# Moving the products behind two attention loops into the loops, pair by pair, and halving the unread products

## The chip, the cores and the metric

The kernel runs on one core of a Trainium2 chip. The metric is the device time of one execution in microseconds (us). The core's engines work beside one another and wait on semaphores: TensorE (PE: matrix products and transposes, with its weight loads, PEld), VectorE (DVE), ScalarE (ACT), GpSimd (POOL) and SyncE (SP, here only the issuer of DMAs). In the profile one float32 product appears as two records on PE; a transpose as one.

## The reference

Four decoder layers over x (16 batches of 112 tokens of 256 elements; 1792 tokens in all) with a context of 375 tokens for each batch:

```python
for l in range(4):
    x = x + tanh(g_xattn[l]) * xattn_l(layernorm(x), ctx, ...)
    x = x + tanh(g_ffn[l]) * ffn_l(layernorm(x), ...)
```

Layers 2 and 3 have attention with 16 heads of 16 elements (layer 2 with rotary positions, layer 3 with a mask) and then a mixture of experts:

```python
# layer 2: attn @ Wo.T + bo; then, with xn = rms_norm(layernorm(x)) * ln_w
logits = xn @ Wg + bg                      # 8 experts, the best 2, softmax over them
y = silu(xn @ W1a_e + b1a_e) * (xn @ W1b_e + b1b_e) @ W2_e + b2_e
# layer 3: attn @ Wo.T + bo; then, with xn = layernorm(x)
scores = sigmoid(xn @ gate.T + bias)       # 9 experts, the best 2, scaled to sum 1
y = silu(xn @ w1_e.T) * (xn @ w3_e.T) @ w2_e.T
```

## The kernel before

All x stays in SBUF as 14 tiles of 128 tokens (`x`, 128 partitions by 14 by 256). `hT` holds 256 by 1792 values with the features on the partitions: normed rows before an attention, and the attention's outcome after it, in the same place. The framework schedules instructions of an engine out of program order where dependencies allow, except those that are pinned (`pinned`, `tc.keep_in_program_order`), which keep their order. Each engine then runs its queue in order.

**The loop `attention16` (L726)** serves layers 2 (tag a2) and 3 (a3). It has 64 units, four heads each of one batch, and 70 steps: step s makes the score products of unit s (`scores`, into one PSUM tile `sS` of four banks with a single buffer) and DVE takes their maxima (layer 2: one reduce; layer 3: four operations that add the mask, L770). A step later the maxima are transposed and subtracted from the queries (`maxima`, qa). `by_keys` makes the scores again, transposed, in rounds of three heads, into the PSUM tag `sT` (three banks, one buffer), and ACT takes their exponentials (L797). Four rounds fall on every three steps: where s % 3 is 1 there are two rounds, one ahead of `values` and one behind it; in other steps one, behind it. `values` works on unit s - 4, then come `by_queries`, `normalise` (sums and o on DVE) and, in even steps, `by_rows`, whose ACT copy (L830) puts 128 rows of 112 tokens into `hT`. Batch b is complete in step 4b + 8. PE's work, and the reduces on DVE, are pinned. The order of a step is written out by hand:

```python
scores(s); tasks of between[s]; by_keys(slot 0); values(s - 4); by_keys(slot 1)
by_queries(s - 4); maxima(s - 1); by_rows; normalise(s - 4); tasks of behind[s]
```

`between` and `behind` are lists of tasks by step. Before the change they hold, for steps 0 to 12 alone, what is left of the norm of the attention's own input: `moments_at` (mean and variance of tiles), `roots_at` (`inv_sqrt`, L187: 12 small DVE operations for 1/sqrt), `scaled_at` (rows minus mean, times root), `rows_at` (PE transposes of a pair of tiles, ACT copies to `hT`) and `group2`/`group3` (queries of four batches). A task of `between` takes its PSUM bank from `sT`.

**Unread products** (`spin`, L256) are products that nothing reads. They stand in six steps at the start of the loop (`spins`), in every step from 64 on (L862: six each), ahead of layer 1's experts (`spin1`), of layer 3's attention (`spin3`, `a3spin`), and in layer 3's routing (`spin4`, and L968 in `dispatch`).

**Behind the loop** `outcome` (L891) goes over groups of four tiles: outcome products with wo (`a2ops`, `a3ops`), DVE's gated add to x (L900), and `norm2` or `norm3` (statistics, root by ACT's square root and DVE's reciprocal, rows kept in `hx`, transposes and copies to `hT`). After all 14 tiles rows (and in layer 3 x) are stored to DRAM for the experts' gather, `route` (L335) makes the router's products for all tiles in one bank, and `chosen`, `softmax_of` and `dispatch` sort tokens into blocks of 256. The expert blocks follow. In layer 2 this stretch also holds 40 fillers (`fill`): keys and values of ten batches for layer 3, each with its loads and stores.

Of the kernel before, what the change touches and what calls it, by code (L numbers as in the profile page):

```python
# [21 lines left out]
P = 128  # L22
# [64 lines left out]
def flamingo_kernel(ctx, tc, a, out):  # L87
# [118 lines left out]
    def roots(n0, m, pin=free):  # L206
        inv_sqrt(rss[:, n0:n0 + m], mvs[:, n0:n0 + m, 1], LN_EPS, pin=pin)

    def norm_stats(n0, m, by_act=False, rms=False):


        moments(n0, m)
        rs, var = rss[:, n0:n0 + m], mvs[:, n0:n0 + m, 1]
        if by_act:
            up, eps = (1.0 + FEPS, FEPS * LN_EPS) if rms else (1.0, LN_EPS)
            nc.vector.tensor_scalar(rs, var, up, eps, ALU.mult, ALU.add)
            nc.scalar.activation(rs, rs, AF.Sqrt)
            nc.vector.reciprocal(rs, rs)
        else:
            roots(n0, m)  # L220
# [113 lines left out]

    def route(name, w, E):  # L335

        ps = ps_o(name)
        for n in range(NT):
            mm2(ps[:, n * E:(n + 1) * E], lambda k: hT[:, k, n * P:(n + 1) * P], w)
        return ps[:, :NT * E]  # L340
# [378 lines left out]
    def rows_at(n):  # L719
        def task(three, mm, tr):  # L720
            ps = three()
            for i in range(2):
                norm_rows(n + i, lambda _: ps[:, i, :], tr, h=hs.pop(n + i))
        return task

    def attention16(pool, pp, tag, qT, kTs, vs_, store, nm=None, maskT=None, beside=(), between=None, behind=None, spins=(0, 0)):  # L726
# [4 lines left out]
        units = 4 * NB  # L731
        oT = hT
# [108 lines left out]
        for s in range(units + 6):  # L841
# [3 lines left out]
            for i, t in enumerate((between or {}).get(s, ())):  # L845
# [15 lines left out]
            if s >= units:  # L861
                spin(mi[:, M_END:], 6, None, mm)  # L862
            for t in (behind or {}).get(s, ()):
                t()
# [25 lines left out]

    def outcome(tag, wo, g, norm):  # L891

        for n0 in range(0, NT, 4):
            m = min(4, NT - n0)
            ps = ps_pair(f"{tag}ops{n0}").rearrange("p i (j d) -> p (i j) d", j=2)[:, :m, :]
            for i in range(m):
                mm2(ps[:, i, :], lambda k: hT[:, k, (n0 + i) * P:(n0 + i + 1) * P],
                    lambda k: wo[:, k, :])
            xs = x[:, n0:n0 + m, :]
            nc.vector.scalar_tensor_tensor(xs, ps, g, xs, ALU.mult, ALU.add)  # L900
            norm(n0, m)
            fill()
# [38 lines left out]
    def dispatch(pool, keep, tag, one, two, gates, n_e):  # L941
# [25 lines left out]
        if not filler:  # L967
            spin(ps_o(f"{tag}spin")[:, :w], 40, tot.rearrange("p e n -> p (e n)"))  # L968
# [460 lines left out]
    both = const.tile([P, NT, 16], F32, name="both")  # L1429
# [124 lines left out]
    spin(ps_pair("spin1")[:, 0, :], 16)  # L1554
    for n in added:
        normed(n, 1, ps_pt)
    for n in turned + added:
        route1(n, ps_o)
# [79 lines left out]
    wo = w3(w_l2o, 0, D)  # L1638
    with tc.tile_pool(name="l2x", bufs=2) as pool:
# [4 lines left out]
        with tc.tile_pool(name="a2ps", bufs=1, space=PSUM) as pp:  # L1644
            attention16(
                pool, pp, "a2", a2qT, a2k, a2v, store_2, beside=prepare,
                between={
                    0: [moments_at(8, 4)], 2: [rows_at(8)], 3: [rows_at(10), moments_at(12, 2)],
                    5: [group2(2)], 6: [rows_at(12)], 8: [group2(3)],
                },  # L1650
                behind={
                    0: [roots_at(8, 4)], 1: [scaled_at(8)], 2: [scaled_at(10)],
                    4: [roots_at(12, 2)], 5: [scaled_at(12)],
                },
# [9 lines left out]
    with tc.tile_pool(name="l2k", bufs=1) as keep:  # L1664
        with tc.tile_pool(name="l2r", bufs=2) as pool:
            hx = pool.tile([P, NT, D], F32, name="hx", bufs=1)

            def norm2(n0, m):
                norm_stats(n0, m, True, True)
                for n in range(n0, n0 + m):  # L1670
                    norm_rows(n, ps_pt, scale_by="lnw", keep=hx)
                    fill()

            outcome("a2", wo, g_x(2), norm2)
            for n in range(NT):
                nc.sync.dma_start(store2[0][n * P:(n + 1) * P, :], hx[:, n, :])
            rp = route("r2", lambda k: cmat("wg", k, E2), E2)
            lg = pool.tile([P, NT, E2], F32, name="lg", bufs=1)
            nc.vector.tensor_tensor(
# [343 lines left out]
```

## Time and profile before

| | us |
|---|---|
| median of 3 runs | 3036.14 |
| lowest, highest run | 3036.07, 3043.58 |
| profiled execution | 3037.71 |
| its span, first to last instruction | 3035.9 |
| layer 2: first scores, last `hT` copy of the loop, first expert product | 1448.8, 1736.3, 1854.1 |
| layer 3: first scores, last `hT` copy of the loop, first expert product | 2302.4, 2638.4, 2707.5 |

PE is busy 94% of the span (2846.5 us), DVE 51%, ACT 34%, POOL 8%; the mean granted clock of PE is 0.966. A line of the timeline gives start, duration, engine, line of the kernel, operation, output and inputs by name with the shape, and how many records are merged into it; in brackets stand the idle time of the engine just before it and what ended that.

### The profile page before, as it was taken

How to read it: one execution, taken by the hardware profiler on the slowest of the kernel's cores; microseconds unless marked ns; L12 is line 12 of the kernel's file. 1: busy time of each engine (PE TensorE's matmuls, PEld its weight loads, DVE VectorE, ACT ScalarE, POOL GpSimd, SP SyncE). 2: the span in 40 equal slices, each digit the busy share in tenths (PEclk: the TensorE clock that was granted, in tenths of full speed). 3: DMA queues.
4: the chain of work that ended last, by engine and by line, in shares of the span. 5: the costliest groups of instructions: out<-in, count | busy, mean ns of one | idle time of the engine just before them, and what ended most of it. 6: DMA issues, size and time to landing. Idle time of an engine off the chain costs nothing. (4 is left out here: it accounts for less than half of the span.)

```text
span 3035.9 us, 50579 instructions
## 1 busy us (share of the span) xinstructions
PE 2846.5 (94%) x20023; PEld 2025.3 (67%) x20023; DVE 1560.3 (51%) x4470; ACT 1045.6 (34%) x2404; POOL 249.2 (8%) x260
## 2 busy tenths in 40 slices
PE   6998999999999999999788898999998899899997
PEld 4666876566666666655555676888875555687775
DVE  5677874466666666656666343222224555342221
ACT  3456973244444444412244331111111333211111
POOL 1000000100000000000000001222210000012321
PEclk9999999999999999999899797999999999889999
DMA  4011334412112111010122156554531222045553
GB/s 166 27 32 59 108 118 156 164 56 65 58 53 65 60 32 40 20 49 7 37 82 86 40 174 217 160 186 157 187 83 45 71 66 65 18 146 149 160 155 96
DMA packets 118866, 282.00 MB, mean 93 GB/s; under 512 B 26904, under 2 KB 86664, under 8 KB 109712
## 3 DMA queue, kind: packets, MB, share of 16 engines
q1 hardware_dynamic: 95920, 242.50, 23.6%
q0 software_dynamic: 19040, 31.83, 5.1%
q10 hardware_dynamic: 3664, 4.37, 0.4%
q8 instruction: 161, 2.64, 0.4%
q14 instruction: 81, 0.66, 0.1%
HBM read 214.92 MB, written 81.35 MB: 98 GB/s over the span
## 5 line engine op out<-in xcount | busy, mean ns | idle before, releaser
L254 PE MATMUL b3ab<-b3xT,w 128*128 128x256 f32 (+1 forms) x864 | 195.5, 385 | 0.5 <-DVE b3xT L1092 0.5
L1108 ACT ACTIVATE b2gs<-b2ab,bias 128x256 f32<-128x256 f32 x144 | 68.2, 473 | 328.1 <-PE b2ab L254 288.1
L254 PEld LDWEIGHTS b3ab<-b3xT,w 128*128 128x128 f32 (+1 forms) x864 | 154.8, 183 | 38.8 <-issue 11.6
L1109 DVE SCALAR_TENSOR_TENSOR b2hid<-b2ab,bias,b2gs 128x256 f32<-128x256 f32 x144 | 69.3, 481 | 201.9 <-ACT b2gs L1108 201.9
L383 PE MATMUL a1vps<-w_l1v,a1cb 128*125 128x512 f32 x360 | 172.1, 602 | 0.9
L383 PE MATMUL a1kps<-a1cb,w_l1k 128*128 128x375 f32 x480 | 165.2, 486 | 0.0
L475 ACT ACTIVATE a1pe<-a1pe,a1mx 112x375 f32<-112x375 f32 x256 | 153.3, 603 | 0.0
L254 PE MATMUL b2ab<-b2xT,wa 128*128 128x256 f32 x576 | 150.4, 384 | 1.4 <-issue 1.4
L254 PE MATMUL b2ab<-b2xT,wb 128*128 128x256 f32 x576 | 148.9, 381 | 0.0
L465 DVE CUSTOM_DVE_ANT_0 a1pe<-a1sc,nm 112x375 f32<-112x375 f32 x256 | 126.0, 544 | 43.9 <-PE a1sc L383 43.9
L770 DVE CUSTOM_DVE_ANT_0 a3ms<-a3sc,first_cb 112x375 f32<-112x375 f32 x256 | 125.1, 545 | 33.8 <-PE a3sc L747 31.7
L386 PEld LDWEIGHTS a1tp<-ident,a1pe 112*125 112x125 f32 x768 | 98.4, 188 | 58.2 <-issue 41.3
L1119 PE MATMUL b2yo<-wc,b2hid 128*128 128x256 f32 x576 | 132.3, 382 | 2.5 <-DVE b2y L1124 0.6
L1114 DVE TENSOR_TENSOR b3hid<-b3ab,b3gs 128x256 f32<-128x256 f32 x108 | 45.7, 424 | 171.7 <-ACT b3gs L1113 171.7
L1113 ACT ACTIVATE b3gs<-b3ab 128x256 f32<-128x256 f32 x108 | 41.3, 382 | 260.1 <-PE b3ab L254 233.5
L797 ACT ACTIVATE a3pT<-a3st 125x1008 f32<-125x1008 f32 x86 | 86.3, 1004 | 122.8 <-PE a3st L747 122.8
L254 PEld LDWEIGHTS b2ab<-b2xT,wa 128*128 128x128 f32 x576 | 110.8, 193 | 17.2 <-issue 2.0
L1119 PEld LDWEIGHTS b2yo<-wc,b2hid 128*128 128x128 f32 x576 | 108.0, 190 | 20.6 <-DVE b2y L1124 6.4
L254 PEld LDWEIGHTS b2ab<-b2xT,wb 128*128 128x128 f32 x576 | 110.4, 192 | 15.2
L766 DVE TENSOR_REDUCE a2mx<-a2sc 112x4 f32<-112x1500 f32 x64 | 110.2, 1722 | 19.0 <-PE a2sc L747 17.1
L383 PEld LDWEIGHTS a1kps<-a1cb,w_l1k 128*128 128x128 f32 x480 | 85.9, 190 | 49.0 <-DVE a1pT L389 3.3
L797 ACT ACTIVATE a2pT<-a2st 125x1008 f32<-125x1008 f32 x86 | 86.3, 1004 | 73.9 <-PE a2st L747 73.9
(469 smaller groups left out, 5706.6 us busy)
## 6 DMA issues: line engine op xcount, KB each, us to landing
w<-all_w SPq DMA_DIRECT2D x36, 704.0 KB
wa<-in_w_l2e1a SPq DMA_DIRECT2D x18, 1024.0 KB
wb<-in_w_l2e1b SPq DMA_DIRECT2D x18, 1024.0 KB
wc<-in_w_l2e SPq DMA_DIRECT2D x18, 1024.0 KB
all_w<-in_w SPq DMA_DIRECT2D x24, 704.0 KB
a2vs<-k2v SPq DMA_DIRECT2D x16, 750.0 KB
a2v<-a2vs SPq DMA_DIRECT2D x16, 750.0 KB
a3v<-a3vs SPq DMA_DIRECT2D x16, 750.0 KB
```

The source lines that it names most:

```text
L254: (mm or nc.tensor.matmul)(dst, lhs(k), rhs(k), start=(k == 0), stop=(k == 1))
L383: pin(nc.tensor.matmul(*args, **kw))
L386: pin(nc.tensor.transpose(*args))
L465: pin(nc.vector.tensor_tensor_reduce(pe[:, 2 * p + j, :], sc[:S, j, :KV], made["nm"], 1.0, FMAX, ALU.add, ALU.min, mx[:, j:j + 1],))
L475: pin(nc.scalar.activation(e, sc[:S, j, :KV] if mask_of is None else e, AF.Exp, bias=mx[:, j:j + 1], scale=1.0 if mask_of is None else -1. ...
L766: pinned(nc.vector.tensor_reduce(mx[:, :, 16], sc[:S, :, :KV], AX.X, ALU.min))
L770: pinned(nc.vector.tensor_tensor_reduce(ms, sc[:S, j, :KV], nm, 1.0, FMAX, ALU.add, ALU.min, mx[:, j, 16:17]))
L797: nc.scalar.activation(pT[:, :n, :], st[:KC, :n, :3 * S], AF.Exp)
L1108: nc.scalar.activation(s[:fn], pa, AF.Silu, bias=bias(0, f))
L1109: nc.vector.scalar_tensor_tensor(hid[:fn, f, :], pb, bias(1, f), s[:fn], ALU.add, ALU.mult)
L1114: nc.vector.tensor_tensor(hid[:fn, f, :], pb, s[:fn], ALU.mult)
L1119: nc.tensor.matmul(po[:, i * D:(i + 1) * D], hid[:fn, f, i * P:(i + 1) * P], w2[:fn, f, :], start=(f == 0), stop=(f == nf - 1),)
```

## The change

For six of the seven pairs of tiles, the outcome products, the gated add, the norm, the stores and the router's products move into the loop, as tasks of a class `Outcome`. For pair n the outcome products and the add are in steps 21, 26, 33, 45, 53, 62, with the moments behind them; roots, scaled rows and stores are behind the next step; transposes are in steps 24, 29, 36, 48, 56, 65, the router's products in 27, 30, 38, 50, 57, 66. The last pair follows the loop (`rest`), with 16 fillers spread over it in layer 2. Roots are DVE's `inv_sqrt` in place of ACT's square root. The router's sums go into `both`, a tile of layer 1. Unread products: none in steps 64 to 69; `spin1` 16 to 8, `spin3` 22 to 13, `a3spin` 16 to 10, `spin4` 12 to 10, `dispatch` 40 to 30. In layer 1 the router's products of tiles already turned are put ahead of `spin1`.

```diff
+    def roots(n0, m, pin=free, rms=False):
+        rs, var = rss[:, n0:n0 + m], mvs[:, n0:n0 + m, 1]
+        if rms:
+            pin(nc.vector.tensor_scalar(rs, var, 1.0 + FEPS, None, ALU.mult))
+        inv_sqrt(rs, rs if rms else var, FEPS * LN_EPS if rms else LN_EPS, pin=pin)
...
+    class Outcome:
...
+        def add(self, n, ps, mm=None, pin=free):
+            for i in range(2):
+                mm2(ps[:, i, :D], lambda k: hT[:, k, (n + i) * P:(n + i + 1) * P],
+                    lambda k: self.wo[:, k, :], mm)
+            xs = x[:, n:n + 2, :]
+            pin(nc.vector.scalar_tensor_tensor(xs, ps[:, :2, :D], self.g, xs, ALU.mult, ALU.add))
+        def scale(self, n, pin=free):
+            roots(n, 2, pin, self.rms)
+            for i in range(n, n + 2):
+                hs[i] = scaled(i, pin)
+                nc.sync.dma_start(self.store[0][i * P:(i + 1) * P, :], hs[i])
+                if self.with_x:
+                    nc.sync.dma_start(self.store[1][i * P:(i + 1) * P, :], x[:, i, :])
+        def route(self, n, ps, mm=None, pin=free):
...
+                        ps[:, 16 * i:16 * i + E], hT[:, k, (n + i) * P:(n + i + 1) * P],
+                        self.w(k), start=k == 0, stop=k == 1,
...
+            pin(nc.vector.tensor_tensor(
+                both[:, n:n + 2, :E], ps[:, :32].rearrange("p (i e) -> p i e", i=2)[:, :, :E],
+                self.bias.unsqueeze(1).to_broadcast([P, 2, E]), ALU.add,
+            ))
+        def tasks(self, between, behind):
+            for n, at, turn, route in zip(
+                    range(0, NT - 2, 2), (21, 26, 33, 45, 53, 62), (24, 29, 36, 48, 56, 65),
+                    (27, 30, 38, 50, 57, 66)):
+                between.setdefault(at, []).append(
+                    lambda three, mm, tr, n=n: self.add(n, three(), mm, pinned))
+                behind.setdefault(at, []).append(moments_at(n, 2))
+                behind.setdefault(at + 1, []).append(lambda n=n: self.scale(n, pinned))
+                between.setdefault(turn, []).append(rows_at(n, self.scale_by))
+                between.setdefault(route, []).append(
+                    lambda three, mm, tr, n=n: self.route(n, three()[:, 0, :], mm, pinned))
+            return between, behind
+        def rest(self, tag):
+            n = NT - 2
+            self.add(n, ps_pair(f"{tag}ops"))
+            fill(4)
+            moments(n, 2)
+            self.scale(n)
+            for i in range(n, n + 2):
+                norm_rows(i, ps_pt, scale_by=self.scale_by, h=hs.pop(i))
+            fill(4)
+            self.route(n, ps_o(f"{tag}r"))
+            fill(8)
...
-            if s >= units:
-                spin(mi[:, M_END:], 6, None, mm)
...
-            spin(ps_o(f"{tag}spin")[:, :w], 40, tot.rearrange("p e n -> p (e n)"))
+            spin(ps_o(f"{tag}spin")[:, :w], 30, tot.rearrange("p e n -> p (e n)"))
...
-    spin(ps_pair("spin1")[:, 0, :], 16)
+    for n in turned:
+        route1(n, ps_o)
+    spin(ps_pair("spin1")[:, 0, :], 8)
...
-            outcome("a2", wo, g_x(2), norm2)
...
-            rp = route("r2", lambda k: cmat("wg", k, E2), E2)
...
+            outcome2.rest("a2")
+            lg = both[:, :, :E2]
...
-        spin(ps_pair("spin3")[:, 0, :], 22)
+        spin(ps_pair("spin3")[:, 0, :], 13)
...
-                spins=(8, 16),
+                spins=(8, 10),
...
-            outcome("a3", wo3, g_x(3), norm3)
...
-            rp = route("r3", lambda k: cmat("wgate", k, E3), E3)
-            spin(ps_mm("spin4")[:, :256], 12, hT[:, 1, T - 256:])
+            outcome3.rest("a3")
+            spin(ps_mm("spin4")[:, :256], 10, hT[:, 1, T - 256:])
```

## The prediction

> **What bounds the kernel now.** I read the page first (span 3035.9 us, PE busy 94%), then the windows by stage, the timeline of both attention loops engine by engine, the chain that ended last, and the lines behind each loop. The windows (span of window, then busy us of PE, PEld, DVE, ACT, POOL; granted clock, DMA share, GB/s) show three regimes of the stages that the diff touches:
>
> ```profile
> 1570.00:1620.00 50.00, 44.35 (x815) 28.84 (x811) 32.55 (x57) 23.62 (x40) 0.00 (x0) 1.00 0.26 80
> ...
> 1722.00:1737.00 15.00, 12.80 (x91) 10.79 (x92) 0.81 (x4) 1.46 (x5) 2.69 (x2) 0.50 0.25 72
> ...
> 1737.00:1742.00 5.00, 4.94 (x25) 4.78 (x24) 0.00 (x0) 0.00 (x0) 0.00 (x0) 0.50 0.33 122
> ...
> 1742.00:1843.00 101.00, 95.12 (x396) 73.47 (x397) 34.58 (x101) 31.35 (x75) 0.00 (x0) 0.85 0.50 178
> ...
> 2644.00:2676.00 32.00, 30.77 (x142) 27.03 (x141) 16.07 (x54) 7.01 (x19) 0.00 (x0) 0.71 0.34 116
> ```
>
> Row 1: the layer 2 loop is full on PE (89%) with DVE at 65%. Rows 2 and 3: its last steps; PE is busy, mostly with unread products, at clock 0.50. Rows 4 and 5: the stretches behind the loops that the change empties, PE full again. Reading the starts of the score products in the timeline, the loops run in a fixed pattern. Where a step has one round of `by_keys` it takes 2.89 (odd) or 3.51 us (even) in layer 2 and 3.46 or 4.08 in layer 3; with two rounds 3.9 or 4.9, and 5.2 or 5.9. One odd step of layer 2:
>
> ```profile
> 1604.73 0.90 PE L747 MATMUL a2sc<-a2kT,a2qT 32*112 32x375 f32 x8
> 1605.71 0.78 PE L747 MATMUL a2mi<-a2pT,a2v 125*32 125x112 f32 x24
> 1606.42 0.92 PE L747 MATMUL a2st<-a2qa,a2kT 32*125 32x112 f32 x18
> 1607.62 0.90 PE L747 MATMUL a2sc<-a2kT,a2qT 32*112 32x375 f32 x8
> ...
> 1605.70 1.72 DVE L766 TENSOR_REDUCE a2mx<-a2sc 112x4 f32<-112x1500 f32 x1
> ```
>
> PE has no gap over 0.1 us here. The reduce (DVE) ends at 1607.42, 0.2 us before the next scores, which need its bank (`sS`, one buffer): nothing pinned on DVE ahead of a reduce is free in such a step.
>
> **Removed.** (a) Unread products of steps 64 to 69. Layer 2, from each run's start to the next useful product: 2.69 + 2.73 + 2.69 + 2.60, then 5.41 behind the last `hT` copy: 16.1 us, all on the chain. Layer 3: 1.44 + 1.47 + 1.60 + 2.60 + 5.41 = 12.5; but there the clock still stood between 0.59 and 1.00, and at half clock the value products take 1.35 instead of 0.78 us, four times, with some `by_keys` beside them: less 3, so 9.5 (6 to 12.5).
>
> (b) Layer 3 behind the loop, from the first `a3ops` to the router's sum:
>
> ```profile
> 2644.15 9.72 PE a3ops L254 x32
> ...
> 2665.65 2.36 PE r L254 x12
> ...
> 2674.20 1.88 PE r L254 x8
> 2676.08 7.29 PE spin L259 x24
> ```
>
> 31.96 us now. What stays is one pair: 8 matmul records at half clock 3.4, the add 0.75, moments 1.1, Newton roots 12 x 0.2 = 2.4, two `scaled` 0.75, transposes and copies 1.3, 8 router records at half clock 1.9, the sum 0.3, hand-overs 0.4: 12.3. Saved 19.7 (16 to 22). `spin4` and the 30 instead of 40 in `dispatch` lie beside DVE's choice and scan (6.7 us up to `sel`): nothing; were `spin4` wholly at half clock, 20 x 0.43 = 8.6, it would cost 1.9.
>
> (c) Layer 2 behind the loop, 1741.98 to the last slot product at 1842.94: 101.0 us, and here PE also makes keys and values of layer 3 (the fillers). At full clock its records cost 80 x 0.315 + 120 x 0.216 = 51.1 for fillers, 12.1 outcome, 3.1 transposes, 6.4 router, 6.4 slots: 79.1; the other 22 are half clock and waits. Without six of seven pairs 60.6 is left; scaled by 101/79.1 that is 77.4, taken as 78: saved 23. Best: 61 (40 saved). Worst: its 18.2 MB (178 GB/s), less 1.6 MB of rows stored early, at the same rate: 92 (9 saved); the densest window shows 264 GB/s, hence nearer the middle.
>
> (d) Start of layer 3. `spin3` is 44 records of 0.4345 and ends 7 us after the rows that it waits beside are ready:
>
> ```profile
> 2262.65 19.12 PE L259 MATMUL spin<-rows,ident 128*128 128x512 f32 x44 [1.17 <-DVEq L1144]
> ...
> 2273.66 1.04 DVE L224 TENSOR_SCALAR h<-x,mvs,rss 128x256 f32<-128x256 f32 x3
> ...
> 2281.61 0.60 PE L236 MATMUL tp<-ident,h 128*128 128x128 f32 x4
> ```
>
> 26 records end at 2273.95: the transposes start 7.4 us sooner. `a3spin` loses 12 x 0.437 = 5.2 us, but the first scores need the queries' DMA, which queues on SP behind value loads that run to about 2290: some 4 us of the 12.6 come back as waits, 1 as a colder first step. Saved 7 (3 to 12.6). `spin1`: its chain is on DVE (`h` at 1312.40, after the spin's end at 1311.0): nothing (0 to 1).
>
> Sum of savings: 16.1 + 9.5 + 19.7 + 23 + 7 = 75.3.
>
> **Added in the loops, per pair.** All four tasks fall on one-round steps, in front of `values`.
> - Outcome: 8 records x 0.216 = 1.73 on PE, in the one `sT` bank. DVE's add (0.75) is queued behind the step's reduce (layer 2) or four mask operations of 0.47 (layer 3), and `by_keys` waits for the bank; `values` covers part. Step +1.86, layer 3 +2.16.
> - Turning: layer 3 has this task already, two tiles in one bank, the second waiting for the first one's copy:
>
> ```profile
> 2345.18 0.41 PE L750 MATMUL a3bt<-ident,h 128*128 128x128 f32 x2 [0.37 <-DVE h L224]
> 2346.05 0.44 PE L750 MATMUL a3bt<-ident,h 128*128 128x128 f32 x2 [0.46 <-ACT hT L245]
> ```
>
> That step takes 5.74 where its like takes 4.08: +1.65; layer 2, with scaled copies of about 0.29 each, +1.55.
> - Router: 8 records x 0.115 = 0.92, then DVE's sum behind the reduce: +1.45, layer 3 +1.7.
> - Roots and `scaled`, pinned behind the next step's work, so in front of the following reduce: 12 x 0.2 (13 in layer 2) + 0.7 = 3.2 us of DVE. The trace has such a case at the start of layer 2, where roots hold a reduce and the scores wait for its bank:
>
> ```profile
> 1457.22 0.16 DVE L197 SCALAR_TENSOR_TENSOR t<-t,v 128x4 f32<-128x4 f32 x1
> 1457.41 0.16 DVE L198 SCALAR_TENSOR_TENSOR rss<-t,rss 128x4 f32<-128x4 f32 x1
> 1457.49 1.71 DVE L766 TENSOR_REDUCE a2mx<-a2sc 112x4 f32<-112x1500 f32 x1
> ...
> 1459.26 1.61 PE L747 MATMUL a2sc<-a2kT,a2qT 32*112 32x375 f32 x8 [2.81 <-DVE a2mx L766]
> ```
>
> For pairs at 21, 33 and 45 the late reduce falls in an odd one-round step: it starts 4.1 instead of 0.97 us into the step and ends at 5.87, the step is 2.89: PE stalls 2.98 (layer 3: 5.9 less 3.46 = 2.44). For pairs at 26 and 53 it falls in a two-round step, which covers more: 1.5 and 1.96 (0.5 and 0.6). The pair at 62 falls into the drain: nothing, and its turning and routing at 65 and 66 cost about 0.8 each.
> - Moments (1.1) delay a reduce in a two-round step, which covers them (1.1 a pair if not). The stores of rows (two or four DMAs a pair) go to SP, where the next batch's keys are four or more steps early: nothing; uncovered, a late key would cost its landing, some 2 us. POOL's queue gets nothing.
>
> Layer 2: 3 x (1.86 + 2.98 + 1.55 + 1.45) + 6.4 + 6.8 + 3.5 = 40.2. Layer 3: 3 x 7.95 + 6.0 + 6.1 + 3.8 = 39.8.
>
> The clock: after PE idled 2.81 us the scores above took 1.61 instead of 0.90, and after 1.69 us idle (at 1508.86) 1.52; half clock then lasted 3 to 9 us. Of the ten stalls, the six long ones, and some of the rest, should do the same at about 1.7 us each: 12 (0 to 24). Row 3 shows 0.50 with PE 99% busy on unread products: there they did not hold the clock, so layer 2 is charged nothing for their loss. [...]
>
> Sum: +40.2 + 39.8 + 12 - 75.3 = +16.7. The profiled execution took 3037.7 us (span 3035.9), 1.6 above the median of the runs; on the median, 3036.1 + 16.7 = **3053**.
>
> **Rivals.** A measurement of this kernel tells about 0.3%, 9 us, from no change.
> - Bursts hidden (faster): if the roots find idle DVE time ahead of the reduce instead of delaying it, the stalls (12.4 + 8.4) and the clock's 12 vanish: +16.7 - 32.8 = -16, 3020. For it: DVE idles 35% of the loop. Against: the rows at 1457. It decides once a scale step's excess is under about 1.3 us a pair.
> - Clock holds (no change): stalls but no half clock: 3041. For it: 1.00 in all the middle of both loops.
> - Fillers bind (slower yet): layer 2's stretch stays at 92: +14, 3067. For it: ACT waits 10.5 us there on stores of values (`a3vs`).
>
> **How the numbers follow.** Forecast 0.41; hidden bursts 0.24 (faster); clock holds 0.20 (same); fillers bind 0.15 (slower). Faster 0.24, same 0.20, slower 0.56. The range 3016 to 3080 takes in most of the first rival below (its best case, with (c) at 40 saved, is 3003) and above it the forecast with the clock's 24 and the third rival; it leaves out about 0.1 on each side. The slower cases' own range is 3046 to 3080.
>
> **What would show it.** Layer 2's loop longer by about 45 us and layer 3's by 45 up to their last scores; scores at steps 24, 36 and 48 idle about 3 us behind the reduce; clock under 1.00 in windows of both loops; `both` complete some 12 us behind the last `hT` copy of layer 3; layer 2's slots ended some 80 us behind its own. Steps 24, 36, 48 on time, or a layer 2 stretch near 65, would make it wrong towards faster.

## The result, and the profile after

The changed kernel takes 3130.9 us (median of 4 runs, 3111.6 to 3142.6) against 3038.4 for the kernel before: 1.0296 times as long, 95% interval 1.0241 to 1.0351. The prediction said slower, 3053 us, with a range up to 3080: the sign was right, and the time lies 51 us above the range.

The profiled execution of the changed kernel took 3142.6 us (span 3140.7), 104.8 us more span than before's. The starts of the score products split it. Layer 2's loop, first to last scores, grew from 255.9 to 341.4 us (+85.5), layer 3's from 307.7 to 383.8 (+76.1); all else together saved 57. The windows of the same stretches as in the prediction, in the same columns (window, then its length, busy us of PE, PEld, DVE, ACT, POOL; granted clock, DMA share, GB/s):

```profile
1580.00:1630.00 50.00, 46.85 (x490) 31.60 (x485) 22.74 (x51) 14.12 (x25) 0.00 (x0) 0.57 0.15 46
1800.00:1812.00 12.00, 10.12 (x91) 7.56 (x88) 1.46 (x7) 4.03 (x9) 0.00 (x0) 0.50 0.07 23
1817.00:1906.00 89.00, 76.92 (x276) 55.06 (x277) 22.08 (x67) 22.23 (x46) 0.76 (x1) 0.81 0.56 202
2768.00:2787.00 19.00, 13.94 (x42) 10.82 (x42) 10.51 (x40) 1.23 (x4) 0.00 (x0) 0.63 0.09 28
```

Row 1 is the middle of layer 2's loop. PE is busier than before (94% of the window against 89%), and yet it works through 490 records in the time in which it worked through 815: the clock is at 0.57 where it was 1.00. A busy share says nothing of this; the count and the clock do. Row 2 lies in that loop's last steps, now without unread products, at half clock. Rows 3 and 4 are the emptied stretches behind the loops: 88.7 us (from `a2ops` to the last slot product) where 101.0 had been, and 18.8 (from `a3ops` to the count over tokens) where 39.3 had been.

Where it begins, in the timeline of PE and DVE (start, duration, and in brackets the idle time before it and who ended it). `scale` has put its burst ahead of the reduce of step 23:

```profile
1569.76 0.74 DVE L226 TENSOR_SCALAR h<-x,mvs,rss 128x256 f32<-128x256 f32 x2
1570.41 1.72 DVE L825 TENSOR_REDUCE a2mx<-a2sc 112x4 f32<-112x1500 f32 x1
1572.18 0.90 PE L806 MATMUL a2sc<-a2kT,a2qT 32*112 32x375 f32 x8 [2.78 <-DVE a2mx L825]
1573.01 0.44 PE L809 MATMUL a2bt<-ident,h 128*128 128x128 f32 x2
1574.17 0.69 PE L809 MATMUL a2bt<-ident,h 128*128 128x128 f32 x2 [0.71 <-ACT hT L241]
1574.79 1.35 PE L806 MATMUL a2mi<-a2pT,a2v 125*32 125x112 f32 x24
1579.07 1.61 PE L806 MATMUL a2sc<-a2kT,a2qT 32*112 32x375 f32 x8
```

The late reduce and the gap of 2.78 us are as predicted. The scores behind the gap still run at full clock (0.90). Two microseconds later, in the step with the turned rows, the same 24 records of value products take 1.35 instead of 0.78 and the next scores 1.61 instead of 0.90: half clock. The prediction expected that too, for 3 to 9 us. It stays, with one break of 7 us, until about 1638, some 65 us later.

Step by step, the time over before's shows two kinds of it. Where the clock is full it is the predicted price: step 21 (outcome) +1.98 in both layers, step 23 (late reduce) +2.85 and +2.31, the same at 35 and 47. Steps in which nothing is added at all are long as well, at half clock: 25, 31, 37 and 49 of layer 2 by 2.2 to 2.3 us each, 31 and 37 of layer 3 by 3.3 to 3.4.

### The profile page after: what moved, and what is told of

Its sections match the earlier page's. It is cut to its first block, busy times and chain, and to the rows that moved or that the text cites. A ratio compares the mean times of both kernels' runs of the same rounds, so it can differ in the third digit from the quotient of the medians.

```text
span 3140.7 us, 50268 instructions
## 1 busy us (share of the span) xinstructions
PE 2902.1 (92%) x19809; PEld 2044.3 (65%) x19809; DVE 1586.0 (50%) x4647; ACT 1042.4 (33%) x2392; POOL 249.2 (8%) x260
```

## Experiments

Excess means the time from step 20 to the last scores less that of before, in the profiled execution: 85.4 us in layer 2 and 74.2 in layer 3 for the changed kernel. Ratios are to the kernel before, run on the same chip, with 95% intervals.

| run | ratio | excess, layer 2 | layer 3 |
|---|---|---|---|
| changed kernel | 1.0296 (1.0241 to 1.0351) | 85.4 | 74.2 |
| e1 stalls alone | 1.0100 (1.0064 to 1.0136) | 22.5 | 7.3 |
| e2 no roots, no copies | 1.0136 (1.0097 to 1.0174) | 37.2 | 29.3 |
| e3 unread products kept | 1.0422 (1.0347 to 1.0496) | 85.6 | 44.2 |
| e4 unread products only | 0.9876 (0.9839 to 0.9912) | 0.0 | 0.0 |
| e5 stalls filled | 1.0136 (1.0104 to 1.0167) | 57.9 | 37.1 |
| e6 own columns | 1.0423 (1.0387 to 1.0459) | 102.5 | 93.8 |
| e7 own columns, spread | 1.0250 (1.0220 to 1.0279) | 64.8 | 63.4 |
| e8 count sooner | 1.0297 (1.0260 to 1.0335) | 85.7 | 65.9 |
| e9 spread | 0.9960 (0.9936 to 0.9985) | 22.1 | 21.5 |
| e10 unread only, start filled | 0.9836 (0.9806 to 0.9865) | 0.0 | 0.1 |
| e11 gap ladder (one run) | 1.0121 | 28.5 | 23.6 |
| e12 gap filled, wide | 1.0121 (1.0080 to 1.0163) | 46.8 | 42.8 |
| e13 gap filled, narrow | 1.0224 (1.0179 to 1.0268) | 64.5 | 50.9 |
| e14 wide behind the gap | 1.0191 (1.0153 to 1.0228) | 66.7 | 54.7 |
| e15 narrow behind the gap | 1.0449 (1.0382 to 1.0516) | 103.6 | 98.9 |

The excess is that of one execution. Between steps 20 and 63 the loops of e3 and e8 are those of the changed kernel, and yet layer 3's excess is 44.2, 65.9 and 74.2 in the three: differences of this size between two rows say little by themselves.

### The late reduce alone, and the tasks alone

e1 gives before the burst and nothing else:

```diff
             for t in (behind or {}).get(s, ()):
                 t()
+            if s in (22, 27, 34, 46, 54):
+                burst()      # inv_sqrt of two columns, two scaled copies, all pinned, into scratch
```

> The kernel before, with nothing of the change but the VectorE burst: behind steps 22, 27, 34, 46 and 54 of both attention loops, 12 small root operations and two scaled copies into scratch, whose results nobody reads, pinned where the change has them. No work is added on TensorE. Theory A (the late reduce stalls the score products, the granted clock falls to half, and stays there for tens of us): about 100 us slower than before, since the two loops of the changed kernel are 85.5 + 76.1 = 161.6 us longer and its tasks account for about 59 of that by their durations at full clock; clock under 0.75 in windows that begin at steps 24, 36 and 48. Theory B (half clock after a stall lasts 3 to 9 us, as the prediction had it, and it is the tasks' own products and waits on TensorE that keep it): 12.4 + 8.4 us of stalls and 10 times 1.7 us of clock, about 38 us slower, with the clock back at 1.00 two or three steps after each burst.

Measured: 29 us slower, near theory B's 38 and far from A's 100. In layer 3 every stall cost its length (a gap of 2.12 us, three times) and the clock held. In layer 2 it fell behind the bursts of steps 22 and 46 (gaps of 2.45) and stayed down for 13.7 us each time, with falls of 3.4 us behind those of steps 27 and 34. The steps at half clock cost some 12 us together.

e2 gives the changed kernel without it:

```diff
         def scale(self, n, pin=free):
-            roots(n, 2, pin, self.rms)
+            if pin is free:
+                roots(n, 2, pin, self.rms)
             for i in range(n, n + 2):
-                hs[i] = scaled(i, pin)
+                hs[i] = scaled(i, pin) if pin is free else x[:, i, :]
```

> The changed kernel without the roots and the scaled copies of the six pairs in the loops (the rows that are turned, stored and routed there are not normalised; all else, the outcome's products and sum, the moments, the turning and the router's products, stays where it is). Theory A: no late reduce, so no stall and no half clock; the loops are longer than before only by the tasks' own 28 and 31 us, and the time is about 103 us under the changed kernel's, near 3030. Theory B: only the stalls' 21 us and some clock go; 3095 to 3110, with the clock in the loops still between 0.5 and 0.8 for most of the time behind step 21.

Its whole time can't be read: rows that are not normalised are routed to other experts, and layer 3's blocks took 120 activations instead of 108 and 47 us more. Its loops can. Apart from one fall in each layer that begins at step 27 (27.3 us of half clock in layer 2, 6.8 in layer 3) each task cost its full-clock price: 1.98 for the outcome, 1.58 and 1.25 for the turning, 1.2 to 1.5 for the router. The fall has a wait ahead of it. The moments that follow the outcome of step 26 delay the reduce of step 27, the router's sum is queued on DVE behind that reduce, and `by_keys` waits for its bank, 1.05 us in layer 2 and 1.30 in layer 3:

```profile
1602.36 1.56 PE L807 MATMUL a2st<-a2qa,a2kT 32*125 32x112 f32 x18 [1.05 <-DVE both L754]
```

So neither theory stood. Stalls alone give 22.5 + 7.3, tasks alone 37.2 + 29.3: 96 together. The changed kernel has 159.6, and the same loops in e3 and e8 129.8 and 151.6. The other 34 to 63 us belong to the two meeting.

### Taking the meeting apart

e5 was to leave the late reduces and fill the gaps (shortened):

```diff
+            n_fill = {23: 3, 35: 3, 47: 3, 28: 1, 55: 1}.get(s, 0)   # layer 3: 23, 35, 47 only
+            if n_fill:
+                st = pp.tile([P, 3, 512], F32, tag="sT", ...)
+                spin(st[:, 0, :384], n_fill, None, mm)
             if s < units:
                 scores(s)
```

> The changed kernel with unread products (128x384 columns, about 0.65 us each at full clock) in front of the score products that the late reduce holds up: three at steps 23, 35 and 47 of both loops, one at 28 and 55 of layer 2. The scores come no sooner, but TensorE idles under 1 us there instead of about 2.8. Theory A (TensorE's idle time brings the clock down: the gap of the late reduce and the waits of the tasks together): the clock behaves as without the roots and copies; from step 20 on layer 2's loop is about 37 + 14 = 51 us longer than before instead of 85, layer 3's about 29 + 9 = 38 instead of 74; the time is about 70 us under the changed kernel's. Theory B (it is not the idle time; any late step does it, or the added work): within 15 us of the changed kernel, the clock behind steps 23, 35 and 47 at about 0.6 as there.

The place needs a word. Counted by the score products that wait, the late reduce of step 23 holds up those of step 24. The filling products stand ahead of step 23's own scores and delay these, and the burst passes meanwhile; the gaps ahead of steps 24, 36 and 48 shrank to 0 to 0.7 us.

Measured: 1.6% under the changed kernel's ratio, about 49 us where theory A had 70; layer 3's excess as theory A had it, layer 2's 7 us more. One thing didn't fit it. In two of the six long places the clock fell although no gap was above 0.5 us, and in a third, step 36 of layer 2, behind two gaps of 0.7 us, for 27 us. The windows around the filling products of layer 2's step 23, whose six records began at 1567.53 and ran on without a gap:

```profile
1567.00:1568.00 1.00, 0.79 (x2) 0.52 (x3) 0.31 (x2) 0.73 (x2) 0.00 (x0) 0.85 0.17 42
1568.00:1571.00 3.00, 3.00 (x6) 1.35 (x4) 2.52 (x16) 0.00 (x0) 0.00 (x0) 0.50 0.00 0
1571.00:1576.00 5.00, 4.37 (x63) 2.25 (x62) 3.67 (x7) 1.86 (x4) 0.00 (x0) 0.99 0.29 87
```

PE is busy for all of the second row at half clock; narrower windows put the fall at about 1567.7 and the return at about 1571.1, 3.4 us. So here the clock did not follow what PE did at the moment: it fell 0.2 us after the products had begun, and came back 3.4 us later with PE as busy as before.

e6 took the turning and the router's products off the shared bank, with the late reduces kept; e7 also spread the DVE work. The lines that both share, shortened:

```diff
-            for i in range(2):
-                norm_rows(n + i, lambda _: ps[:, i, :], tr, scale_by=scale_by, h=hs.pop(n + i))
+            # transposes into columns 376 to 503 of the four banks of this step's scores
+            tr(sc[:, 2 * i + c, 376:376 + P], h[:, c * P:(c + 1) * P], ident)
...
-                    lambda three, mm, tr, n=n: self.route(n, three()[:, 0, :], mm, pinned))
+                    lambda three, mm, tr, n=n: self.route(n, mi[:, M_END:], mm, pinned))
```

> The changed kernel with the turning and the router's products of the pairs written to columns that are free in the banks of the scores and of the maxima, so that these two tasks no longer wait for the one bank that they share with by_keys; the outcome's products stay in that bank, and the late reduces stay. Theory A1 (the tasks' own waits keep the clock down after a late reduce has lowered it): the loops come near to stalls alone plus the tasks' products, 22.5 + 20 in layer 2 and 7.3 + 20 in layer 3 instead of 85 and 74: some 90 us under the changed kernel. Theory A2 (the gap of the late reduce is enough by itself once there is any task near it): 5 to 25 us under the changed kernel, with the clock still near 0.6 behind steps 23, 35 and 47.

> The changed kernel with both: own columns for the turning and the router's products as in the run before, and the moments, roots and scaled copies of a pair handed out operation by operation over the steps that follow the outcome, as many as the step's reduce leaves time for (1.4 us in a step with two rounds of by_keys, 0.6 in an even one with one round, none in an odd one). Nothing is left out. Outcomes at 21, 27, 33, 45, 54 and 62, turnings at 32, 41, 50, 59, 65 and 67. If late reduces and the tasks' waits are all of the cause: no stall, no half clock, loops longer by the products alone, about 2.0 + 0.6 + 0.9 us a pair, 20 us each, and a time of about 3131 - 65 - 54 = 3012. If the added products alone lower the clock: 3050 to 3090.

Both missed. The transposes now waited for the reduce that reads those banks, as the timeline of e7 at step 32 shows:

```profile
1610.66 0.44 PE L886 MATMUL a2sc<-ident,h 128*128 128x128 f32 x2 [2.11 <-DVE a2mx L903]
```

The edit put a wait of 2.1 us ahead of each turning, so it did not test what it was meant to. It is a test all the same: with one more gap a pair e6 took 39 us more than the changed kernel (1.0423 less 1.0296, times 3040), and the spreading alone, with a gap at each turning, did not save the loops (64.8 and 63.4).

e9 is e7 with the tasks in the shared bank again. Its core:

```diff
-                behind.setdefault(at, []).append(moments_at(n, 2))
-                behind.setdefault(at + 1, []).append(lambda n=n: self.scale(n, pinned))
+            room = (0.6, 1.4, 0.6, 0.0, 1.4, 0.0)       # us free ahead of a step's reduce, by s % 6
+            ...                                         # pieces: moments 0.55, a root operation 0.2, a copy 0.38
+                left = 9.0 if s >= 63 else room[(s + 1) % 6] - (0.75 if s in ats else 0.0)
+                while queue and queue[0][0] <= left:    # hand out pieces while they fit
```

> The changed kernel with the moments, roots and scaled copies handed out over the steps as in the spread kernel, and the turning and the router's products in the shared bank, where the change has them (the free columns of the scores' banks had put 2.1 us of waiting for the reduce ahead of each turning). Nothing is left out. If late reduces are what tips the clock, and the tasks' own short waits alone do not: loops longer by about 2.0 + 1.6 + 1.3 us a pair, 25 to 30 us each from step 20 on, against 85 and 74 in the changed kernel, the clock at 1.00 for nearly all steps: about 3131 - 57 - 46 = 3028. If the tasks' waits alone bring it down as well: loops 50 to 65 us longer, 3070 to 3110.

Measured: 0.9960 of before, some 102 us under the changed kernel (1.0296 less 0.9960, times 3040); the excess is 22.1 and 21.5, somewhat under the 25 to 30 expected, since a pair's last tasks fall into the drain. The windows of both loops from 1540 and 2390 on:

```profile
1540.00:1736.00 196.00, 173.21 (x2924) 114.66 (x2916) 132.94 (x293) 86.89 (x154) 0.00 (x0) 1.00 0.23 71
2390.00:2634.00 244.00, 219.75 (x3270) 143.01 (x3268) 148.72 (x647) 88.18 (x152) 0.00 (x0) 1.00 0.22 68
```

The clock is 1.00 throughout, with DVE busier than in the changed kernel and PE less: 88% and 90%. All of the moved work is there, with the tasks' own waits, and it costs what its products and short waits cost. But e9 differs in two ways: the late reduces are gone, and the tasks stand in other steps (outcomes at 27 and 54 instead of 26 and 53, and all turnings and router's products later). It doesn't show how much of the 102 us belongs to each. e2, without late reduces but with the tasks in the changed kernel's steps, still had its falls behind the waits of step 27; in e9 no wait of PE from step 20 to the last scores is above 0.72 us.

### How long a gap, and what comes behind it

e11 pins 3, 4, 5, 6, 7, 8 and 10 scaled copies ahead of the reduces of steps 23 to 59 of before, six steps apart:

```diff
+            for n in range({22: 3, 28: 4, 34: 5, 40: 6, 46: 7, 52: 8, 58: 10}.get(s, 0)):
+                scaled(n, pinned)
```

> The kernel before with nothing but scaled copies (0.37 us of VectorE each, into scratch, read by nobody) pinned ahead of the reduce of steps 23, 29, 35, 41, 47, 53 and 59 of both loops: 3, 4, 5, 6, 7, 8 and 10 of them. TensorE's gaps should grow from about 0.9 to 3.5 us in layer 2 and from 0.5 to 3.1 in layer 3. If it is the length of one gap that counts: each step up to some length costs its gap and nothing more, and from that length on (2.3 to 2.8 us by the runs so far, where layer 3's 2.19 never and layer 2's 2.52 mostly did it) the steps behind it cost 4 to 8 us more at half clock. If any gap does it at random: extra time behind short gaps as often as behind long ones.

The held-up scores of layer 2 (timeline of PE):

```profile
1563.92 0.90 PE L747 MATMUL a2sc<-a2kT,a2qT 32*112 32x375 f32 x8 [1.26 <-DVE a2mx L766]
1586.37 0.90 PE L747 MATMUL a2sc<-a2kT,a2qT 32*112 32x375 f32 x8 [0.85 <-DVE a2mx L766]
1609.16 0.90 PE L747 MATMUL a2sc<-a2kT,a2qT 32*112 32x375 f32 x8 [1.18 <-DVE a2mx L766]
1632.45 0.90 PE L747 MATMUL a2sc<-a2kT,a2qT 32*112 32x375 f32 x8 [1.50 <-DVE a2mx L766]
1661.27 1.61 PE L747 MATMUL a2sc<-a2kT,a2qT 32*112 32x375 f32 x8 [1.82 <-DVE a2mx L766]
1688.64 1.61 PE L747 MATMUL a2sc<-a2kT,a2qT 32*112 32x375 f32 x8 [2.15 <-DVE a2mx L766]
1716.68 1.61 PE L747 MATMUL a2sc<-a2kT,a2qT 32*112 32x375 f32 x8 [2.79 <-DVE a2mx L766]
```

Up to 1.26 us a step cost its gap. Behind 1.50 us three further steps cost 5.3 us more, and from 1.82 on the scores right behind the gap are already at half clock (1.61). In layer 3 the gaps of 0.93, 0.52, 0.84 and 1.49 cost themselves, 1.17 cost 1.55 more, 1.81 and 2.46 cost 6.9 and 5.2 more. So the length counts, but with no sharp edge: e1's 2.12 us in layer 3 never did it. And without tasks nearby a fall cost 1.6 to 6.9 us in all.

What blurs the edge is where the gap lies. In all 17 profiles every change of the granted clock inside the span falls on one grid of 3.413 us, to within 0.003 us over the whole 3 ms; only the place of the grid differs from execution to execution. These are the cells of the grid at two late reduces of layer 3: of e1, whose gap of 2.12 us is cut by an edge, then of e11, whose gap of 1.81 lies in one cell.

```profile
2459.28:2462.69 3.41, 2.61 (x51) 1.83 (x47) 3.03 (x17) 1.26 (x2) 0.00 (x0) 1.00 0.16 44
2462.69:2466.11 3.42, 2.02 (x35) 1.16 (x35) 2.82 (x14) 0.25 (x1) 0.00 (x0) 1.00 0.32 132
```

```profile
2596.16:2599.57 3.41, 1.60 (x25) 0.75 (x19) 3.06 (x14) 1.01 (x1) 0.00 (x0) 1.00 0.17 44
2599.57:2602.99 3.42, 3.42 (x46) 2.54 (x45) 1.96 (x8) 0.25 (x1) 0.00 (x0) 0.50 0.03 6
```

PE was busy for 77% and 59% of e1's two cells, and the clock held; it was busy for 47% of e11's first, and the clock fell at that cell's end. Over the loops of all profiles, from step 20 on, the clock fell behind every one of the 52 cells at full clock with PE busy for less than 55%, behind 39 of the 113 with 55 to 75%, and behind 7 of the 1481 with more. e1's three gaps in layer 3 are 54.6 us apart, 16 cells, so the grid cut them all alike: they are one draw, not three.

e12 and e13 put dense unread products beside the late reduces, wide or narrow, of the same duration:

```diff
             if s < units:
                 scores(s)
+            if s in (23, 28, 35, 47, 55):
+                spin(st[:, 0, :384], 4, None, mm)       # e12; st is a tile of the shared bank
+                spin(mi[:, M_END:], 12, None, mm)       # e13, in its place: 48 columns
```

> The changed kernel with every late reduce and its gap left as it is, and four unread products of 128x384 columns (2.9 us at full clock, 5.2 at half) right behind the held-up scores of steps 23, 28, 35, 47 and 55 of both loops. Theory C (the gap tips the clock for one window of some 3.4 us, and what keeps it down afterwards is that the loop's own small products with their waits are too little work; dense wide products bring it back): half clock ends within 3.4 to 7 us of the gap, so each loop is about 12 (stalls) + 5 x 4 (the added products) + 27 (the tasks) = 60 us longer from step 20 on in layer 2 and 55 in layer 3, against 85 and 74 in the changed kernel: about 40 us under it in spite of the added work. Theory A as first stated (only idle time counts, and the gaps are all there): no better clock, and the added products on top, 25 to 40 us over the changed kernel.

> The same, but with twelve unread products of 128x48 columns (5.5 us at half clock, the shape of those in the drain of the kernel before) in place of the four wide ones. TensorE is as busy and idles as little as in the wide run. Theory C, if it is work in the array and not busy time that counts: the clock stays down as in the drain of before (0.50 at 99% busy), so 30 to 50 us over the changed kernel. If busy time alone brings the clock back: as the wide run, about 30 to 40 us under the changed kernel.

The edit did not do what these texts say. Behind the scores of step 23 means ahead of the gap, which the next step's scores close: the products filled it (the gaps at 24, 36 and 48 shrank to 0.15 us or nothing). So read, both are a cleaner e5. At these three steps of both layers the clock read 1.00 throughout the next 13 us in all 12 places, wide and narrow alike; in the changed kernel it fell in all 6, and in e3 and e8 in all 12. The 13 us from the scores of layer 2's step 24 on, of e12 and then of the changed kernel:

```profile
1570.23:1583.23 13.00, 11.24 (x173) 7.43 (x176) 7.72 (x13) 5.74 (x12) 0.00 (x0) 1.00 0.31 90
```

```profile
1572.18:1585.18 13.00, 11.84 (x127) 8.09 (x127) 4.57 (x8) 4.37 (x10) 0.00 (x0) 0.55 0.18 62
```

The steps were as long as ever (+2.85 at 23 in layer 2). In these places it was not the late scores that brought the clock down but PE standing still. At step 27 the clock fell in both runs and both layers, behind the waits of 1.05 and 1.30 us that e2 has there too, and then the two parted. Behind the wide products of step 28 it was back 6.8 us after the fall, in both layers; behind the narrow ones after 37.5 and 23.9. By their ratios e12 and e13 are 53 and 22 us faster than the changed kernel; only the first is clear of the intervals.

e14 and e15 leave the gaps and follow them: the same products behind the held-up scores themselves.

```diff
-            if s in (23, 28, 35, 47, 55):
+            if s in (24, 29, 36, 48, 56):
```

> The two runs before put their products behind the scores of steps 23, 28, 35, 47 and 55, and the scores that a late reduce holds up are those of the next step: so they filled the gap of 2.3 to 2.9 us instead of following it. Here the four wide products (128x384) stand behind the held-up scores themselves, at steps 24, 29, 36, 48 and 56, and the gaps stay. Theory C (gap and short waits together tip the clock, wide work brings it back): the clock falls at some of these steps for 3.4 to 7 us and then holds; excess from step 20 on about 55 to 65 us in layer 2 and 50 to 60 in layer 3 (stalls 12 and 8, tasks 30, added products 10 to 20). If wide work right behind the gap prevents the fall: excess about 12 + 30 + 10 = 52 and 48, with 1.00 behind steps 24, 36 and 48. If nothing but the gap counts: as the changed kernel and more, 90 to 105.

> The same with twelve narrow products (128x48) behind the held-up scores of steps 24, 29, 36, 48 and 56. Theory C with work in the array as the measure: the gap tips the clock, the narrow products do not bring it back, and at half clock they take 5.4 us each time: excess 95 to 115 us in layer 2 and 85 to 100 in layer 3, 20 to 50 us slower than the changed kernel. If any dense work behind the gap prevents or ends the fall: as the wide run within 10 us.

Windows from the held-up scores of layer 2's step 24 on, of e14 and then of e15:

```profile
1578.40:1585.40 7.00, 6.66 (x18) 3.04 (x18) 2.21 (x4) 0.20 (x1) 0.00 (x0) 0.62 0.19 76
1585.40:1605.40 20.00, 16.99 (x276) 11.80 (x280) 10.40 (x28) 7.67 (x16) 0.00 (x0) 1.00 0.13 39
```

```profile
1589.70:1596.70 7.00, 6.92 (x33) 5.85 (x34) 2.24 (x5) 0.00 (x0) 0.00 (x0) 0.50 0.20 74
1596.70:1613.70 17.00, 15.85 (x155) 10.65 (x158) 5.09 (x9) 5.04 (x10) 0.00 (x0) 0.54 0.09 25
```

The gap before both is 2.78 us, and in both the clock falls within it. In e14 it is back before the seven microseconds are over, and the next 20 us run at 1.00 with all of the tasks in them. In e15 PE is as busy and stays at half. The other places agree. With the wide products the clock fell at five of the six long gaps and at steps 29 and 56 of layer 2, and the half clock lasted 3.4 us in four of the seven places and 6.8 in three: one or two cells of the grid. (It also fell at step 38 of layer 2 and step 27 of layer 3, with no late reduce before and no wide products behind, for 3.4 and 6.8.) With the narrow ones it fell at all six long gaps and stayed down for 17 to 51 us. With neither, in the changed kernel, e3 and e8, falls at these gaps lasted 3.4 to 34 us, 15 of 18 of them over 7. The excess is 66.7 and 54.7 for the wide (theory C: 55 to 65 and 50 to 60) and 103.6 and 98.9 for the narrow (95 to 115 and 85 to 100). e14 is faster than the changed kernel by 1.05% (32 us) with 41 us of added products in its two loops.

### The unread products and layer 2's stretch

e3 puts all unread products back into the changed kernel, e4 takes them out of before and changes nothing else:

```diff
+            if s >= units:                              # e3; taken out in e4
+                spin(mi[:, M_END:], 6, None, mm)
-        spin(ps_pair("spin3")[:, 0, :], 13)
+        spin(ps_pair("spin3")[:, 0, :], 22)             # and 16, 40, 16, 12 for 8, 30, 10, 10
```

> The changed kernel with all of the unread products of before put back (steps 64 to 69 of both loops, 16 at layer 1, 22 and 16 at the start of layer 3, 40 and 12 behind layer 3's loop). The prediction's terms: they lie on the path, so 16.1 + 9.5 + 7 = 33 us slower than the changed kernel. Rival: at half clock they carry the clock over the last steps and the starts, and taking them away cost about what it saved: within 10 us of the changed kernel, the drain's products and the first steps of layer 3 at a higher clock.

> The kernel before with only the unread products dropped and halved as in the change, and no work moved. The prediction's terms: 16.1 + 9.5 + 7 = 33 us faster than before, near 3005. Rival (the unread products hold the clock, or cover waits that would show up): 0 to 10 us faster, with the time given back in the outcome's products behind layer 2's loop or in layer 3's first steps.

They cost about 38 us in both (1.0422 less 1.0296, where the intervals just overlap, and 1 less 0.9876, times 3040): the prediction's 33 stands, and the loops' falls are there with them as without. In e4's profile the first steps of layer 2 ran at half clock for longer: 17.2 us more over steps 0 to 19 than in the profiled execution of before. e2, e3, e8, e13 and e15 had the same there, e1, e7, e9 and e14 6.6, the changed kernel, e5, e6, e11 and e12 nothing. The unread products have no part in this, e3 has all of them; the place of the grid sorts the profiles. From the start of step 1's scores to the grid's next edge it is 1.35 to 1.66 us in before and the five that lost nothing, 1.76 to 1.96 in the four that lost 6.6, and 2.09 to 2.30 in the six that lost 17. These steps have gaps of 1.8, 3.6 and 3.1 us in e4. e10 fills them:

```diff
+            n_fill = {1: 2, 2: 3}.get(s, 0) if nm is None else 0     # ahead of scores(s)
             if s < units:
                 scores(s)
+            if s == 6 and nm is None:
+                spin(st[:, 0, :384], 3, None, mm)
```

> The kernel before with only the unread products dropped and halved, as run already, and with unread products (128x384 columns, 0.65 us each) in three places at the start of layer 2's loop where TensorE waits for VectorE: two ahead of step 1's scores (gap 1.8 us), three ahead of step 2's (2.8 to 3.6 us), three ahead of step 6's turned rows (3.1 us). If idle gaps bring the clock down: steps 2 to 14, which took 17 us longer in that kernel's profile than in before's, keep full clock, and its time is 5 to 20 us less than that kernel's, a ratio to before of 0.982 to 0.986. If not idle time: the ratio stays at 0.988, with half clock in steps 2 to 14 as often as before.

Windows over the first 59 us of layer 2's loop, of e4 and of e10:

```profile
1453.00:1512.00 59.00, 46.39 (x418) 31.12 (x419) 33.94 (x83) 13.81 (x22) 0.00 (x0) 0.76 0.10 23
```

```profile
1451.00:1510.00 59.00, 49.13 (x532) 31.36 (x535) 41.22 (x97) 16.50 (x28) 0.00 (x0) 0.96 0.14 33
```

The profile shows the cause removed; in the time, 0.9836 against 0.9876 is 12 us, and the two intervals overlap. At 2994.6 us, e10 is the fastest kernel of the study, and it moves no work at all.

e8 takes `fill(8)` out of `rest` and out of `dispatch`, so that the count over tokens no longer stands behind 16 parts of layer 3's keys and values:

> The changed kernel with the 16 parts of layer 3's keys and values that stand between the router's sum and the count over tokens (d2cp) put behind it; they are made before the slots, as the rest of them. If the late d2cp holds up layer 2's stretch: it comes 19 us sooner, and the last slot product 10 to 19 us sooner. If the transfers of those keys and values bind the stretch (the scalar engine's waits on stores, 11 us): 0 to 4 us.

The count came 19.9 us behind `a2ops` instead of 43.6, but the last slot product 84.6 instead of 88.7: the second case. The order is worth 4 us; the stretch is bound by making those keys and values.

## Why the prediction was right or wrong

**Wrong: the clock, 12 us (0 to 24).** This is the step that failed. The two loops' excess is 159.6 us; the prediction's other terms for them make 40.2 + 39.8 = 80.0; so half clock cost 79.6 (some 88 by the full-clock prices that e1, e2 and e9 show). The prediction took "3 to 9 us" of half clock from the start of layer 2 in one execution of before. Its three falls there last 10.2, 10.2 and 3.4 us by the granted clock, and even that was luck in the place of the grid: six of the profiles above lost 17 us more at the same steps. Some seven times 1.7 us then treated the falls as independent of the work behind them. For the stalls alone that was about right: e1's falls cost 12 us. With the tasks around them it was not: the ten falls of the changed kernel's two loops last 7 to 41 us, eight of them 17 or more, 235 us of half clock in all. Shown, in these runs: the gaps of the late reduces tipped the clock at steps 24, 36 and 48, by leaving PE without work and not by the scores being late (filled, in e12 and e13, it read 1.00 in 12 of 12 places); the waits for the router's sum, 1.05 and 1.30 us, tipped it at step 27 without the roots' burst (e2, e12, e13); once it was down, wide products had it back after 3.4 or 6.8 us (e14, 7 of 7), and behind narrow ones it stayed down for 17 to 51 us (e15). (The prediction let two-round steps cover the moments. That holds for the pairs at 21, 33 and 45; those at 26 and 53 meet one-round steps, and the wait of step 27 comes from there.) Not shown: what sets the clock. A cell with PE busy for less than 55% brought the fall 52 times of 52, but between 55 and 75% it came 39 times of 113, and the busy share does not tell which. Columns per product went together here with the share of weight loads (PEld 3.04 us beside 6.66 of PE in e14's seven microseconds, 5.85 beside 6.92 in e15's), and the two were not told apart.

**Right: the price of each task and stall at full clock.** Outcome 1.98 (predicted 1.86 and 2.16). Turning 1.45 to 1.65 in layer 2 and 1.12 to 1.32 in layer 3 (1.55 and 1.65), and router 1.1 to 1.7 (1.45 and 1.7), both in e9, where the clock holds. Late reduce 2.85 and 2.31 (2.98 and 2.44), in the two-round step 55 1.87 and 0.63 (1.96 and 0.6).

**Savings: 75.3 predicted, 61.8 measured.** (a) 13.1 in layer 2 (16.1) and 9.9 in layer 3 (9.5). (b) 20.5 (19.7); the chain of waits behind layer 3's loop is now

```profile
2768.23 3.69 PE a3ops L256 x8
2772.02 0.76 DVE x L735
2777.86 1.88 PE a3r L749 x8
2779.73 7.24 PE spin L261 x20
```

one pair, as worked out. (c) 12.3 instead of 23, inside its 9 to 40 (the 18.2 MB behind that 9 are 18.0 in the trace, which does give its 92): PE now waits 11.1 us for the copies of values (`k3bv`), 5.5 before, so the third rival came true for 10.7 of its 14 us. (d) 6.0 instead of 7, less 2.5 for a first step at half clock: behind 26 spin records the queries' transfer is late, as the prediction had it, by 6.45 us:

```profile
2326.93 11.40 PE L261 MATMUL spin<-rows,ident 128*128 128x512 f32 x26 [1.52 <-DVEq L1188]
2360.29 1.70 PE L806 MATMUL a3sc<-a3kT,a3qT 32*112 32x375 f32 x8 [6.45 <-DMA a3qT<-a3qc]
```

`spin1`, put at 0 to 1, seems to have cost 2.8 us up to layer 2's first scores: with half of it gone PE stands idle for 7.64 us ahead of layer 1's experts, runs at half clock behind that, and the first expert product starts 1.4 us later. No run tests this alone.

Added up on the prediction's +16.7: 67.6 for the clock, 13.5 less saved, 2.8 for `spin1` and 2.5 for layer 3's first step make 103.1, against 104.9 between the two profiled executions.

**The rivals.** Hidden bursts would have given 3020, the prediction said; e9, which hides them, has 0.9960 of before, 3024 on the prediction's 3036.1. The clock did not hold: no gap ahead of the loops' scores from step 20 on was above 2.8 us, and it fell behind gaps of 1.05 (e2) and 1.50 (e11).

## What to carry to other kernels

Price a short stall by what follows it as much as by its length: on this loop of small products with short waits a gap of 2 to 3 us was followed by anything from no half clock (e1's 2.12 us in layer 3) to 13.7 us of it (e1's 2.45 in layer 2), and with the tasks beside it by 3.4 to 34 us (changed kernel, e3, e8); the same work, handed out in pieces that fit the free time of the other engine and in other steps, left the clock at 1.00 (e9). A recovery time read from one place of one execution is no bound: the 3.4 to 10.2 us of before were one place of a grid of 3.413 us, and six other profiles lost 17 us more at the same steps. Look at several executions, and for the place whose following work resembles that of the change. And work moved from behind a full loop into it must still be paid there: even with the late reduces gone (e9), moving the work and dropping the unread products gained less than dropping them alone (0.9960 against 0.9876).

## What was not expected of the hardware

- With PE 94% busy on the loop's small products the clock averaged 0.57 over 50 us (changed kernel), and with PE 99% busy over 7 us, most of it on products of 48 columns, it stayed at 0.50 (e15). Being busy did not bring it back there; 4.5 to 5 us of products of 384 columns did, 7 times of 7, after 3.4 or 6.8 us (e14).
- At full clock the same narrow products were enough to keep it: a gap of 2.2 to 2.8 us filled with either kind left the clock at 1.00 in 12 of 12 places (e12, e13), and behind the gap, at half clock, the narrow ones did not bring it back (e15).
- The clock fell for 3.4 us while PE worked without a gap (e5: 0.50 with PE busy for 3.00 of 3.00 us), 0.2 us after dense work had begun.
- Whether layer 2's first 20 steps lost 0, 6.6 or 17 us went by the place of the 3.413 us grid, without an exception in 16 profiles of kernels that run the same work there.
